# A fused decoder layer: the order of VectorE's, ScalarE's and GpSimd's work from a scheduler with a simulated timeline

## The chip, the cores and the metric

The kernel runs on one core of one Trainium2 chip, as one program. The metric is the device time of that core in microseconds (us); the number for a kernel is the median over several executions. A profile is one further execution taken by the hardware profiler. A core has a matrix engine (TensorE, in the profile PE, its weight loads PEld), VectorE (DVE), ScalarE (ACT), GpSimd (POOL) and a queue that issues DMAs (SP). Each engine works through its own list of instructions in the order in which the program holds them, and the engines meet through semaphores: an instruction waits until the results that it reads are there and the buffers that it writes are free.

## The reference

The program computes one decoder layer in fp32 for `x` of 32 batches x 100 tokens x 256 and a context of 32 x 361 x 256. Cut to what matters:

```python
x = x + self_attention(layernorm(x))        # 16 heads of 16, causal, rotary q and k, @ Wo.T
x = x + cross_attention(layernorm(x), ctx)  # 16 heads of 16, 361 keys, with biases
x = x + soft_moe(layernorm(x))              # below

def soft_moe(x):                            # 8 experts with 128 slots each, hidden size 1024
    xn, sn = rmsnorm(x) * gamma, rmsnorm(slot_embeds) * gamma2
    logits   = einsum('bnd,esd->bnes', xn, sn)
    dispatch = softmax(logits, over tokens n)
    combine  = softmax(logits, over all slots e,s)
    slots = einsum('bnd,bnes->besd', xn, dispatch)
    eo    = gelu(slots @ w1 + b1) @ w2 + b2   # per expert
    return einsum('bmd,bnm->bnd', eo, combine)
```

## The kernel before, in words

The 32 batches are taken in eight groups of four. For each batch there is self-attention, cross-attention and the token normalization; then, for each group, the eight experts run on the four batches' slots together. While the experts of one group run, the attention of the next group's batches is woven in between their matmuls. Only the first group's attention (with the constants) has no experts beside it, and only the last group's experts have no attention beside them. In the profile this gives a start and a preparation of 291 us, six nearly equal periods of 396 us, and an end without attention.

TensorE's order is written out by the kernel itself. Generators (`self_attention`, `cross_inputs`, `cross_softmax`, `prepare`, `route`) yield points in an estimate of TensorE's time, and `between`, called inside `run_expert`, decides which generator may put its next matmuls there. The helpers `matmul` (line 88) and `transpose` (line 92) wrap each TensorE instruction in `tc.keep_in_program_order`, which binds its place. All matmuls therefore appear in the profile under line 88, all transposes under line 92, and are told apart by their tiles.

The instructions of VectorE, ScalarE and GpSimd have no such binding. A scheduler takes the traced program and lays each engine's list out, subject to data and buffers; it also places the semaphore waits.

The steps that the prediction names, by tile and line:

- Start: the context copies `ctxT` (L547) and the slot normalization `sq` (L264, eight squares with a sum each), `n` (L265), `rn` (L267, GpSimd), `se` (L269, eight), `ps_sn` and `snT` (L282). `wTWo` (L202) is a weight turned by TensorE.
- Every layer norm: `bnmv` (L308), then on GpSimd `ve`, `rstd`, `xh` (L310 to L318); TensorE turns it into `ps_xhT`, ScalarE copies that into `xhT` (L330).
- Self-attention: `ps_qk`, then the rotation `ropeu`, `ropet` (L392 to L395, VectorE and GpSimd) and `rotk` (L398, ScalarE); `spad` (L410) holds the values. The scores `sc` are masked into `p` (L430), reduced to `nmax` (L436), shifted on GpSimd (L437), raised by Exp (L441, written `p<-p`), summed (`sums`, L442), inverted (`rinv`, L444) and widened (`wide`, L344). TensorE turns `p` into `ps_pT`, copied to `pT` (L460).
- Cross-attention: `ps_kT` and `kT` (L559), `vpad` (L573), `ps_xq` and `xqT` (L589), scores `xsc`, `xnmax` (L607), Exp `xp` (L611), turned into `ps_xpT` and copied to `xpT` (L627 on ScalarE, L629 on VectorE); `rb` (L354) is the spread inverse of the sums.
- Experts: routing makes `dT` and `cT` (Exp at L824 and L825, `sm` L827, `ri` L829), `disp` (L836) and `slT` (L848); `ph` is the first expert product, Gelu writes `hT` (L873), `pe` is the second product, `eo` (L890) takes it out, `py` combines, and L903 adds it to `x` (called the combine).

PSUM has one tile of four banks for scores, two banks "mm" and two "big", which `ph` and `pe` share with other work; a matmul that needs a bank waits for the copy that empties it.

## Time and profile before

| | |
|---|---|
| median of 3 runs (lowest, highest) | 3293.3 us (3292.8, 3299.66) |
| profiled execution, and its span in the profile | 3290.16 us, 3288.4 us |
| TensorE busy, share of the span | 3080.1 us, 94% |
| ScalarE busy | 1447.5 us, 44% |
| VectorE busy | 1292.9 us, 39% |
| GpSimd busy | 555.5 us, 17% |
| table loads on ScalarE | 272 of 1283 ns |
| mean granted TensorE clock | 0.98 |

How to read it: a busy TensorE does not mean TensorE at its peak, since its matmuls overlap and their ends are modelled. In a line of the profile "out<-in" names the tiles, "x4096" is a count, then come the busy time, the mean of one, and the idle time of that engine just ahead with what ended it. "PE ps_qk L88 <- ACT xhT L330" is TensorE, at the product `ps_qk`, waiting for ScalarE's `xhT`. In a timeline the first number is the start from the span's beginning, the second the duration of the merged pieces, and a bracket holds the idle time before them.

### The profile page before, as it was taken

The page shows a single profiled execution, that of the slowest core. Times are in us where ns is not written, and L with a number is a line of the kernel's source. Part 1 is how long each engine was busy: PE and PEld are TensorE (multiplying, and loading weights), DVE is VectorE, ACT ScalarE, POOL GpSimd, SP SyncE. Part 2 cuts the span into 40 slices and gives each one's busy share as a digit, 9 for nine tenths or more (in the row PEclk, how much of TensorE's full clock was granted, in tenths as well). Part 3 has the DMA queues.
Part 4 walks back from the last instruction along what each step waited for, and adds up shares of the span by engine and source line. Part 5 has one row for each costly group of instructions (what it writes and reads, how often), then busy time and mean ns, then how long its engine had stood idle before and what let it go on. Part 6 is the DMA issues. An engine that isn't in the chain of part 4 may idle for free.

```text
span 3288.4 us, 44719 instructions
## 1 busy us (share of the span) xinstructions
PE 3080.1 (94%) x18481; PEld 2126.4 (65%) x18481; DVE 1292.9 (39%) x2477; ACT 1447.5 (44%) x2824; POOL 555.5 (17%) x816
## 2 busy tenths in 40 slices
PE   5778999999999999999999999999999999999999
PEld 3556666666666666666666666766666666666666
DVE  3554444433443443434443343443443433422211
ACT  2444445344454445444445345444445444534331
POOL 3231211103101121112211011210211102000000
PEclk9788999999999999999999999999999999999999
DMA  3000111111111111112111111112111111111121
GB/s 107 10 10 13 47 49 56 47 51 60 47 45 59 52 45 64 47 43 67 47 45 52 60 45 59 47 45 65 47 45 48 57 48 55 42 63 64 63 64 55
DMA packets 116316, 167.51 MB, mean 51 GB/s; under 512 B 4521, under 2 KB 99729, under 8 KB 116113
## 3 DMA queue, kind: packets, MB, share of 16 engines
q1 hardware_dynamic: 112368, 161.01, 15.1%
q10 hardware_dynamic: 3744, 3.65, 0.4%
q8 instruction: 145, 2.38, 0.3%
q14 instruction: 59, 0.48, 0.0%
HBM read 161.36 MB, written 3.28 MB: 50 GB/s over the span
## 4 chain that ended last, share of the span: by engine, by line
PE 80%; ACT 9%; DVE 5%; POOL 4%; issue 2%; DMA 0%; ACTq 0%; DVEq 0%; POOLq 0%
PE ph L88 24%; PE pe L88 24%; PE sl L88 3%; PE ps_xpT L92 3%; PE xsc L88 3%; PE ps_lt L88 2%; PE ps_xv L88 2%; PE py L88 2%; PE ps_xav L88 2%; PE ps_kT L88 2%; ACT L873 2%; PE ps_o L88 2%; ACT hT L873 2%; POOL p L437 1%; ACT xp L611 1%
## 5 line engine op out<-in xcount | busy, mean ns | idle before, releaser
L88 PE MATMUL pe<-w,hT 128*128 128x256 f32 x4096 | 1048.3, 386 | 1.8 <-ACT hT L873 1.8
L88 PE MATMUL ph<-slT,w 128*128 128x512 f32 x2048 | 994.4, 602 | 25.3 <-ACT hT L873 24.6
L88 PEld LDWEIGHTS pe<-w,hT 128*128 128x128 f32 x4096 | 734.8, 191 | 170.3 <-issue 73.1
L873 ACT ACTIVATE hT<-ph,cols 128x512 f32<-128x512 f32 x512 | 350.3, 687 | 486.7 <-PE ph L88 480.8
L88 PEld LDWEIGHTS ph<-slT,w 128*128 128x128 f32 x2048 | 357.2, 190 | 291.1 <-issue 224.8
L611 ACT ACTIVATE xp<-xsc,xnmax 100x361 f32<-100x361 f32 x512 | 282.9, 558 | 263.6 <-DVE xnmax L607 262.8
L607 DVE TENSOR_REDUCE xnmax<-xsc 100x2 f32<-100x722 f32 x256 | 231.7, 905 | 250.6 <-PE xsc L88 172.8
L92 PEld LDWEIGHTS ps_xpT<-ident,xp 100*128 100x128 f32 (+1 forms) x1536 | 183.7, 157 | 120.9 <-issue 63.3
L629 DVE COPY xpT<-ps_xpT 128x400 f32<-128x400 f32 (+1 forms) x256 | 145.1, 570 | 261.8 <-PE ps_xpT L92 261.2
L830 POOL TENSOR_TENSOR dT<-dT,ri 128x400 f32<-128x400 f32 x64 | 55.3, 864 | 1012.3 <-DVE ri L829 968.5
L92 PE MATMUL ps_xpT<-ident,xp 100*128 100x100 f32 (+1 forms) x1536 | 203.9, 260 | 19.8 <-ACT xp L611 9.6
L873 ACT ACT_TABLE_LOAD x136 | 174.5, 1283 | 83.1 <-PE ph L88 81.3
L890 DVE TENSOR_TENSOR eo<-pe,b 128x512 f32<-128x512 f32 x128 | 88.2, 689 | 279.9 <-PE pe L88 279.3
L823 POOL TENSOR_TENSOR cT<-lt,nmB 128x400 f32<-128x400 f32 x64 | 66.2, 1039 | 679.9 <-ACT nmB L810 354.3
L903 DVE SCALAR_TENSOR_TENSOR x<-py,cinv,x 100x256 f32<-100x256 f32 x256 | 112.1, 479 | 164.5 <-PE py L88 163.6
L88 PEld LDWEIGHTS sl<-disp,xn 100*128 100x128 f32 x1024 | 133.9, 194 | 20.9 <-ACT rb L354 8.0
L88 PE MATMUL sl<-disp,xn 100*128 100x128 f32 x1024 | 137.3, 278 | 9.1 <-ACT rb L354 5.2
L437 POOL TENSOR_TENSOR p<-p,nmax 100x800 f32<-100x800 f32 x64 | 96.1, 1523 | 249.9 <-DVE nmax L436 239.5
L88 PE MATMUL py<-eo,cT 128*100 128x256 f32 x512 | 131.8, 380 | 0.8 <-DVE eo L890 0.8
L88 PE MATMUL xsc<-kT,xqT 32*100 32x361 f32 x1024 | 112.8, 510 | 10.4 <-ACT xp L611 9.5
L848 DVE TENSOR_SCALAR slT<-sl,cols 128x512 f32<-128x512 f32 x128 | 95.5, 746 | 65.0 <-PE sl L88 64.4
L310 POOL TENSOR_SCALAR ve<-bnmv 100x1 f32<-100x1 f32 x96 | 21.4, 223 | 582.7 <-DVE bnmv L308 579.2
(143 smaller groups left out, 3416.6 us busy)
## 6 DMA issues: line engine op xcount, KB each, us to landing
w<-in_L_ffn_w_dram SPq DMA_DIRECT2D x128, 1024.0 KB
ctx<-in_ctx_dram SPq DMA_DIRECT2D x32, 256.0 KB
b<-in_L_ffn_b_dram SPq DMA_DIRECT2D x64, 128.0 KB
ctx<-in_ctx_dram SPq DMA_DIRECT2D x32, 105.0 KB
x<-in_x_dram SPq DMA_DIRECT2D x8, 400.0 KB
out_dram<-x SPq DMA_DIRECT2D x16, 200.0 KB
se<-n_L_ffn_slot_embeds_dram ACTq DMA_DIRECT2D x1, 1024.0 KB
rawWk<-in_L_attn_Wk_dram ACTq DMA_DIRECT2D x1, 256.0 KB
```

The lines of the kernel that those rows point to most:

```text
L88: tc.keep_in_program_order(nc.tensor.matmul(out, lhsT=lhsT, rhs=rhs, **kw))
L92: tc.keep_in_program_order(nc.tensor.transpose(out, in_, identity))
L437: nc.gpsimd.tensor_tensor(p[:, hs, :], p[:, hs, :], nmax[:, hs].unsqueeze(2).to_broadcast([S, HPC, S]), ALU.subtract,)
L607: nc.vector.tensor_reduce(nmax[:, c, q : q + 2, r], sc[:S, q : q + 2, :SK], axis=AX.X, op=ALU.max, negate=True,)
L611: nc.scalar.activation(p[:, q, :], sc[:S, q, :SK], AF.Exp, bias=nmax[:, c, q, r : r + 1], accum_out=sums[:, c, q, r : r + 1],)
L629: nc.vector.tensor_copy(pT[:n], ps[:n, : HG * S])
L823: nc.gpsimd.tensor_tensor(cT, k.lt[e], k.nmB, ALU.add)
L830: nc.gpsimd.tensor_tensor(dT, dT, ri.unsqueeze(2).to_broadcast([P, nb, S]), ALU.mult)
L848: nc.vector.tensor_scalar(slT[:, dc, :], sl[:, : nb * NS], cols[:, NGM + dc : NGM + dc + 1], None, ALU.mult)
L873: nc.scalar.activation(h[:, :n], ph_[:, :n], AF.Gelu, bias=cols[:, e * NHC + hc : e * NHC + hc + 1])
L890: nc.vector.tensor_tensor(eo[:, :m], po[:, :m], b2.unsqueeze(1).to_broadcast([P, m, D]), ALU.add)
L903: nc.vector.scalar_tensor_tensor(xg[g][:, b, :], py[:S, i, :], k.ci[:, b : b + 1], xg[g][:, b, :], ALU.mult, ALU.add,)
```

## The change

One argument at the place where the program is made:

```diff
-    with _tile.TileContext(nc) as tc:
+    with _tile.TileContext(nc, schedule_with_timeline_sim=True) as tc:
         decoder_layer(tc, aps, *outs)
```

With it the scheduler keeps a simulated timeline while it lays the lists out, so that the instruction taken next on an engine follows that timeline's idea of what is ready. The traced program is the same, instruction by instruction. What differs is the order on three engines and, with it, where the semaphore waits stand: TensorE's list is the same; 537 of VectorE's 2445 instructions, 285 of ScalarE's 2017, 425 of GpSimd's 813 and 4 of SP's 280 stand in another place. Four excerpts of ScalarE's list, old and new, with the times that the places had in the profile before:

```
start (20 to 43 us)
  old: ctxT x2, sq x8, xhT, rotk x2, spad, kT x2
  new: ctxT x2, xhT, rotk x2, sq x7, spad, sq, kT x2
preparation (242 to 248 us)
  old: Exp p, Exp p, xhT, xnT, xp, xp
  new: xhT, xnT, xp, xp, Exp p, Exp p
period (345 to 356 us)
  old: hT, xhT, Exp cT, hT, hT, rotk x2, spad
  new: hT, xhT, hT, Exp cT, hT, spad, (hT,) rotk x2
period (517 to 530 us)
  old: hT, xp, xp, ctxT, ctxT, Exp p, xpT, Exp p, kT
  new: hT, ctxT, xp, xp, ctxT, xpT, kT, Exp p, Exp p
```

On VectorE the commonest moves are of neighbours: `xpT` ahead of `nmax` or `sums`, `xqT` or `xnmax` ahead of `wide`, `ri` and `sm` ahead of `slT`, the combine ahead of `nmax`. On GpSimd the short layer norm steps `ve`, `rstd`, `xh` pass the token normalization's chain (L729 to L737), which was interleaved with them.

## The prediction

> **What bounds the kernel now.** I read the busy totals and the chain first, then who TensorE waits for, then the stretches.
>
> ```profile
> PE 3080.1 (94%) x18481; PEld 2126.4 (65%) x18481; DVE 1292.9 (39%) x2477; ACT 1447.5 (44%) x2824; POOL 555.5 (17%) x816
> PE 80%; ACT 9%; DVE 5%; POOL 4%; issue 2%; DMA 0%; ACTq 0%; DVEq 0%; POOLq 0%
> ```
>
> TensorE (PE) is busy 3080.1 of 3288.4 us; 208 us are gaps. Its own work isn't touched, so a gain can only come out of those gaps, and a loss can only be a new gap. The other three engines idle for over half the time: their amount of work doesn't bind, the moment at which each result is ready does. TensorE's waits, longest first (who waits, for whom: us in total, times, longest):
>
> ```profile
> PE ps_qk L88 <- ACT xhT L330: 25.8, 3, 21.8
> PE ph L88 <- ACT hT L873: 24.6, 21, 1.7
> PE ps_l L92 <- ACT ps_l L795: 23.1, 7, 3.6
> PE ps_rb L92 <- DVE wide L344: 13.9, 3, 6.5
> PE ps_xq L88 <- ACT xhT L330: 11.8, 3, 5.3
> ```
>
> Many short waits in many places, and one long one. The stretches (us: TensorE busy, the number of its instructions; then the clock and the DMA columns at the end):
>
> ```profile
> 0.00:57.00 57.00, 22.20 (x153) 17.72 (x153) 19.15 (x41) 12.76 (x35) 17.91 (x31) 0.95 0.48 147
> 57.00:291.00 234.00, 175.38 (x1561) 129.12 (x1554) 135.51 (x267) 102.45 (x288) 71.28 (x103) 0.83 0.03 9
> 687.00:1083.00 396.00, 380.84 (x2307) 262.06 (x2306) 160.65 (x307) 183.29 (x353) 68.61 (x100) 0.99 0.16 52
> 3007.00:3289.00 282.00, 266.65 (x1050) 184.06 (x1050) 51.54 (x97) 83.51 (x106) 13.36 (x14) 1.00 0.19 63
> ```
>
> Gaps: 35 us in the start (7 of them for the first weights' DMAs, 22 at `ps_qk`), 59 us in the first group's preparation, where no expert runs beside it, 15 us in each later period of 396 us, 15 us in the last experts.
>
> [...] on ScalarE `xhT` needed only `ps_xhT`, done at 11.45, and went at 32.89, after eight squares that waited for the DMA of `se`:
>
> ```profile
> 21.86 0.82 ACT L547 COPY ctxT<-ps_cT 128x361 f32<-128x361 f32 x2
> 29.69 0.42 ACT L264 ACTIVATE sq<-se 128x256 f32<-128x256 f32 x1 [7.00 <-DMA se<-n_L_ffn_slot_embeds_dram]
> 32.89 0.30 ACT L330 COPY xhT<-ps_xhT 128x200 f32<-128x200 f32 x1
> ```
>
> [...] the trace has 1283 x272. [...] the trace shows one `wide` copy at 1.13 us against a mean of 0.32, beside GpSimd. A new order can move such clashes; I take zero and keep 0.8 us for each of five to ten either way (4 to 8 us) for the range.
>
> **The change, part by part.** No instruction is added or removed. TensorE's order is the same. Of VectorE's 2445 instructions 537 stand in another place, of ScalarE's 2017 285, of GpSimd's 813 425, most by one to four places; of SP's 280 DMAs 4 (the third ctx load passes x and b, nothing waits there). The 272 table loads stay, with the same number ahead of each line. So cost is only lateness: I keep every TensorE start where the trace has it, lay the other queues out in the new order with each instruction's duration from the trace, starting it when its queue and its inputs are done (handover 0.03 to 0.09 us, as the trace shows), and read how much earlier or later TensorE's operand is than before. The same layout in the old order makes nothing late by over 0.05.
>
> *Start.* `xhT` goes ahead of the squares: 22.7 to 23.0 instead of 33.2, so `ps_qk` and the rotation start 10.3 earlier. The squares now stand behind `rotk` (two, 29.6 to 30.4) and the last one behind `spad`: the chain square, n2, rn (1.67), se (8, 2.19) ends 1.0 later. `ps_sn` follows se directly, its first at 36.4, its last at 39.3 instead of 44.1, so `sc` comes 4.7 earlier. VectorE's `wTWo` (0.68) now stands ahead of `nmax`, hidden again by the earlier `wide`. Kept: 4.4 us.
>
> *Preparation.* The clearest place is 246.6:
>
> ```profile
> 243.97 0.87 ACT L441 ACTIVATE p<-p 100x800 f32<-100x800 f32 x1 [4.37 <-POOL p L437]
> 245.45 0.87 ACT L441 ACTIVATE p<-p 100x800 f32<-100x800 f32 x1 [0.61 <-POOL p L437]
> 246.22 0.31 ACT L330 COPY xhT<-ps_xhT 128x200 f32<-128x200 f32 x1
> ```
>
> `xhT`, ready at 240.2, waited behind two Exps that waited for GpSimd; it now goes first, and the stall of 3.5 us at `ps_qk` goes. At 276.2 `xhT` likewise (2.6, but the second Exp falls behind a `pT` copy and gives 1.7 back: 0.9); at 71.9 the four `xqT` ahead of `sums` and `rinv` (1.5); at 99.5 the cross Exps and their `xnmax` ahead of `pT` and `xqT` (2.7); at 225.2 the same with `rotk` (2.1). Five smaller gains of 0.2 to 0.5: 1.6. Seven losses of 0.1 to 0.8, the largest `ropeu` behind a 0.91 `xnmax` at 221: 2.6. Net 9.7.
>
> *Periods.* The largest gain:
>
> ```profile
> 347.85 1.28 ACT L825 ACT_TABLE_LOAD   x1
> 351.16 0.54 ACT L825 ACTIVATE cT<-cT 128x400 f32<-128x400 f32 x1 [2.02 <-POOL cT L823]
> 351.71 1.28 ACT L873 ACT_TABLE_LOAD   x1
> 353.01 1.26 ACT L873 ACTIVATE hT<-ph,cols 128x512 f32<-128x512 f32 x2
> ```
>
> The first of these two Gelus (its `ph` was done long before) now goes ahead of the Exp that waited for GpSimd, so TensorE's 1.54 stall at 353.7 goes. Beside it:
>
> ```
> place (and each 396 us on)   what passes what                        us, times      sum
> 331  sl                      xnmax ahead of ri                       +0.61 x7      +4.3
> 354  ph                      hT ahead of Exp cT                      +1.53 x6, .94 +10.1
> 434  ps_xpT                  combine x, xpT ahead of nmax, Exp p     +0.92 x6      +5.5
> 521  sc                      two cross Exps sooner                   +0.38 x6      +2.3
> 526  ps_xpT, ps_kT           xpT ahead of nmax and Exp p       +1.7, +0.24 x5      +2.9
> 535  py                      Exp p behind kT, so sums, disp, eo late -1.10 x6      -6.6
> 692  ph                      sm (0.57) ahead of slT                  -0.31 x6      -1.9
> ```
>
> Sum +16.6. The loss at 535: Exp `p` at 526.07 now stands behind `kT`, which waits for `ps_kT` until 528.9, so it and all behind it are 3.3 late; 2.2 of that is covered by slack at `py`:
>
> ```profile
> 526.07 0.87 ACT L441 ACTIVATE p<-p 100x800 f32<-100x800 f32 x1 [4.80 <-POOL p L437]
> 528.89 0.56 ACT L559 ACTIVATE kT<-ps_kT,cols 128x361 f32<-128x361 f32 x1 [0.47 <-PE ps_kT L88]
> ```
>
> *End.* +1.0 at 2854.6 (combine ahead of other work), -0.5 at 2966.3; the last five stalls of 1.67 stay. Net +0.5.
>
> Elsewhere moves cost nothing: `sm`, `ri` ahead of `slT` in about 25 experts lie under 1.2 to 12 us between the second `slT` and its `ph`. The DMAs follow TensorE's progress and are no later relative to it; no TensorE wait after 8.3 us is for a DMA.
>
> Sum: 4.4 + 9.7 + 16.6 + 0.5 = 31.2. Against the profiled execution's 3290.2: 3259. The median of the runs is 3.1 higher: 3262. A gain at one place survives to the next unless a chain begun before it ends within its slack; laying the gains out as earlier TensorE starts, only the losses named came up.
>
> **Rivals.** (a) The gaps come back: TensorE reaches the next operand earlier and waits for it, as in the preparation, where it waits for VectorE, ScalarE and GpSimd in turn. For: its gaps there are a quarter of the time. Against: most chains start at TensorE and move with it. Half kept: 3293 - 16 = 3277. (b) Nothing measurable: the engines are 39% and 44% busy, so order is of no account. Against: the `xhT` line, 22 us at one place in an idle queue. About 3292. (c) Slower: `rotk` (L398) now stands behind `spad` and `hT`, which wait for TensorE, in 19 of 32 batches; it ends up to 2.5 later. For: `sc` waits for it, and all of self-attention behind that. Against: `sc` starts 3.3 to 12.3 after `rotk` ends. Without that cover 19 x 2.5 = 47 against 31: 3293 + 16 = 3309. It decides above (31.2 + 6.6)/19 = 2.0 uncovered each.
>
> **How the numbers follow.** No change is within 0.2% (6.6 us). Forecast 3254 to 3269: 0.72; (a) 3270 to 3282: 0.16; (b) 0.06; (c) 0.06. Forecast and (a) are both faster: 0.88. Range 3250 [...] to 3278 (most of (a)).
>
> **What would show it.** `xhT` at about 23 and `ps_qk` just behind; no stall at 246 or 354; a new one of about 1 us at `py` near 535; TensorE's gaps about 177 instead of 208, its busy time as before. It is wrong if a new wait of `sc` for `rotk` appears, if a period isn't shorter by about 2.3 us, or if gaps in the preparation stay at 59.

## The result, and the profile after

The changed kernel takes 3254.0 us in the median of four runs (3250.9 to 3259.1), the kernel before 3295.6 in the runs beside them: a ratio of 0.9878, with a 95% interval of 0.9861 to 0.9895. The forecast was 3262, the range 3250 to 3278. The profiled execution took 3259.1 us (span 3257.4), and the forecast for it was 3259.

So the profiled execution became 31.0 us shorter and the median 41.6. The kernel before's profiled execution (3290.2) lies 5.5 below its median and the changed one's 5.1 above its own: 31.0 + 5.5 + 5.1 = 41.6. Why one execution stands off its median by that much is taken up under "The start, and the clock".

Busy totals and the shares of the chain that ended last, of the changed kernel:

```profile
PE 3078.0 (94%) x18481; PEld 2119.3 (65%) x18481; DVE 1284.2 (39%) x2477; ACT 1448.9 (44%) x2824; POOL 553.2 (17%) x816
PE 84%; ACT 8%; DVE 5%; issue 2%; POOL 1%; DMA 1%; ACTq 0%; DVEq 0%; POOLq 0%; SPq 0%
```

TensorE's busy time is 2.1 us less than before, its gaps (the time in which it is idle) are 179.4 us (3257.4 - 3078.0) instead of 208.3. GpSimd has gone from 4% of the chain to 1%. TensorE's waits (who, for whom: us in total, times, longest):

```profile
PE ps_l L92 <- ACT ps_l L795: 22.8, 7, 3.6
PE ps_kT L88 <- ACT kT L559: 15.2, 7, 2.5
PE ph L88 <- ACT hT L873: 15.0, 13, 1.7
PE ps_qk L88 <- ACT xhT L330: 14.8, 2, 14.4
PE ps_xq L88 <- ACT xhT L330: 6.0, 3, 5.2
...
PE ps_sn L92 <- DVE se L269: 4.3, 1, 4.3
...
PE ps_xpT L92 <- DVE xqT L589: 2.8, 6, 0.5
```

`ps_qk` has given 11.0 us, `ph` 9.6 (eight waits fewer), `ps_xq` 5.8. New are `ps_sn` for `se` and `ps_xpT` for `xqT`. The two longest rows that come back in every period, `ps_l` (23.1 before) and `ps_kT` (15.2 before), are nearly as they were. At the places at 246, 348 to 353 and 526 to 529 us that the prediction shows of before, ScalarE's timeline now reads (the second Exp of the pair at 246 is merged with the first, at 234.95):

```profile
230.67 0.33 ACT L330 COPY xhT<-ps_xhT 128x200 f32<-128x200 f32 x1 [0.55 <-PE ps_xhT L92]
...
234.95 1.88 ACT L441 ACTIVATE p<-p 100x800 f32<-100x800 f32 x2
...
333.91 0.69 ACT L873 ACTIVATE hT<-ph,cols 128x512 f32<-128x512 f32 x1 [0.56 <-PE ph L88]
334.62 1.28 ACT L825 ACT_TABLE_LOAD   x1
335.91 0.54 ACT L825 ACTIVATE cT<-cT 128x400 f32<-128x400 f32 x1
...
512.45 0.56 ACT L559 ACTIVATE kT<-ps_kT,cols 128x361 f32<-128x361 f32 x1 [3.91 <-PE ps_kT L88]
512.91 1.62 ACT L441 ACTIVATE p<-p 100x800 f32<-100x800 f32 x2
```

`xhT` goes ahead of the Exps. One Gelu passes the Exp of `cT`, and that Exp doesn't wait for GpSimd any more. `p` stands behind `kT` and is late, as forecast. (Below, "the place at 354" means the instructions that stood there in the profile before, and the same ones each 396 us on.) The same stretches as before (us, TensorE busy and number of instructions, then the other engines, the granted clock, DMA):

```profile
0.00:57.00 57.00, 25.58 (x153) 19.71 (x153) 18.65 (x42) 12.15 (x35) 17.88 (x31) 0.89 0.51 147
57.00:291.00 234.00, 184.86 (x1605) 134.07 (x1606) 139.85 (x276) 109.23 (x297) 75.16 (x107) 0.84 0.03 9
687.00:1083.00 396.00, 382.92 (x2315) 262.19 (x2314) 159.49 (x307) 184.50 (x355) 68.41 (x100) 0.99 0.16 52
```

The start has 3.4 us more TensorE busy time, but at a clock of 0.89 instead of 0.95; the preparation has 49 us of gaps instead of 59.

TensorE's list is the same in both kernels, so its idle time can be compared instruction by instruction. In gaps alone (idle time just ahead of each instruction, changed kernel minus kernel before):

```
stretch                         forecast    measured
start (0 to 57)                   -4.4        -3.9   (-7.4 at ps_qk, +4.3 at ps_sn)
preparation (57 to 291)           -9.7        -9.3
six periods                      -15.1       -14.3   (-3.8 in the first, -2.1 in each later one)
the rest                          -2.0        -1.3
sum                              -31.2       -28.8
```

(The forecast's 331 and 354 count a seventh time in the rest: 0.61 + 0.94 of its 16.6, and 0.5 for the end.) Busy time gives the other 2.1.

### The profile page after: what moved, and what is told of

The parts are those of the page before. It is cut to its first block, busy times and chain, and to the rows that moved or that the text cites. A ratio compares the mean times of both kernels' runs of the same rounds, so it can differ in the third digit from the quotient of the medians.

```text
span 3257.4 us, 44717 instructions
## 1 busy us (share of the span) xinstructions
PE 3078.0 (94%) x18481; PEld 2119.3 (65%) x18481; DVE 1284.2 (39%) x2477; ACT 1448.9 (44%) x2824; POOL 553.2 (17%) x816
## 3 DMA queue, kind: packets, MB, share of 16 engines
q1 hardware_dynamic: 112368, 161.01, 15.4%
## 4 chain that ended last, share of the span: by engine, by line
PE 84%; ACT 8%; DVE 5%; issue 2%; POOL 1%; DMA 1%; ACTq 0%; DVEq 0%; POOLq 0%; SPq 0%
PE ph L88 26%; PE pe L88 25%; PE ps_xpT L92 4%; PE sl L88 3%; PE py L88 3%; PE xsc L88 3%; PE ps_lt L88 3%; PE ps_xv L88 2%; PE ps_xav L88 2%; PE ps_kT L88 2%; PE ps_o L88 2%; PE ps_qk L88 2%; ACT L873 1%; ACT hT L873 1%; PE ps_pT L92 1%
## 5 line engine op out<-in xcount | busy, mean ns | idle before, releaser
L823 POOL TENSOR_TENSOR cT<-lt,nmB 128x400 f32<-128x400 f32 x64 | 66.3, 1042 | 661.1 <-ACT nmB L810 345.4
L627 ACT COPY xpT<-ps_xpT 128x400 f32<-128x400 f32 x128 | 62.7, 490 | 176.9 <-PE ps_xpT L92 176.6
L88 PEld LDWEIGHTS py<-eo,cT 128*100 128x100 f32 x512 | 84.9, 167 | 55.6 <-issue 31.6
```

Of the source, the lines that this page charges most:

```text
L88: tc.keep_in_program_order(nc.tensor.matmul(out, lhsT=lhsT, rhs=rhs, **kw))
L627: nc.scalar.copy(pT[:n], ps[:n, : HG * S])
L823: nc.gpsimd.tensor_tensor(cT, k.lt[e], k.nmB, ALU.add)
```

## The experiments

TensorE's list stays the same in all kernels but one, which adds transposes. To set another engine's order, each of the kernels e1 to e11 writes it out and binds every instruction behind the one before it (shortened):

```diff
     with _tile.TileContext(nc) as tc:
         decoder_layer(tc, aps, *outs)
+        for engine, order in ORDERS.items():          # positions in the traced program
+            mine = [i for i in nc.cur_bb.bb.instructions if i.engine == engine]
+            for a, b in zip(order, order[1:]):
+                tc.add_manual_dep(mine[b], mine[a].name, NO_SYNC, reason="pin")
```

The scheduler's timeline is off in them, but for e9 and e12. "Old" and "new" below are the lists of the kernel before and of the changed one. All results together, with two columns that the first experiments called for: TensorE's busy time and gaps in the profiled execution, and the number of steps at half clock in it ("half steps"), counted from 20 us on. Each ratio is against runs of the kernel before that stand beside the kernel's own. (A step is 3.413 us: so long are the shortest whole stretches at 0.5 in the profiles of before and changed, and in the records of the granted clock of every one of these profiles, all stretches at 0.5 from 100 us on begin at whole multiples of 3.413 us from each other, to 0.01 of a step.)

```
kernel                              median    ratio (95%)             span     busy     gaps   half steps
before                              3295.6    1                       3288.4   3080.1   208.3    39
changed                             3254.0    0.9878 (0.9861-0.9895)  3257.4   3078.0   179.4    36
e1  ScalarE new, periods            3300.3    1.0009 (1.0000-1.0018)  3297.0   3091.7   205.3    46
e2  VectorE new, periods            3323.0    1.0073 (1.0047-1.0100)  3312.3   3089.2   223.1    43
e3  GpSimd new, periods             3298.5    1.0002 (0.9992-1.0011)  3297.4   3094.5   202.9    48
e4  all new, preparation            3280.3    0.9945 (0.9925-0.9965)  3278.9   3076.5   202.4    36
e5  ScalarE+VectorE new, periods    3287.1    0.9966 (0.9953-0.9978)  3281.9   3082.9   199.0    43
e6  changed, three places mended    3251.4    0.9863 (0.9846-0.9879)  3247.3   3075.5   171.8    38
e7  changed, two ScalarE moves      3221.0    0.9767 (0.9753-0.9782)  3218.5   3070.9   147.7    31
e8  changed, ps_sn wait filled      3265.3    one run                 3263.4   3086.9   176.4    40
e9  changed, 66 moves               3200.3    0.9714 (0.9700-0.9729)  3197.8   3063.8   134.0    30
e10 before, two ScalarE moves       3258.2    0.9889 (0.9874-0.9903)  3257.7   3077.6   180.1    40
e11 new order, buffers by old rule  3263.1    0.9899 (0.9881-0.9918)  3261.8   3082.5   179.3    41
e12 changed, once more              3258.9    one run                 3257.2   3079.7   177.5    35
```

### One engine at a time, in the periods

e1, ScalarE's list, in each period (all but the place at 434, whose new order needs VectorE's):

```diff
-hT, Exp cT, hT           | rotk x2, spad, hT | xp, xp, ctxT | Exp p, xpT, Exp p, kT
+hT, hT, Exp cT           | spad, hT, rotk x2 | ctxT, xp, xp | xpT, kT, Exp p, Exp p
```

> ScalarE alone in the new order, from 291 us to the end of the periods (2700), all its moved places but the one at 434 (xpT ahead of two Exp p, which VectorE's old order doesn't allow). VectorE, GpSimd and all other stretches in the old order. Theory (ScalarE's order carries the places 354, 521, 526 and the loss at 535): 354 -10.1, 521 -2.3, 526 about -1.5, 535 +6.6, so about 7 us less than the kernel before; TensorE's wait of ph for hT at 354 is gone and py at 535 waits about 1 us. Rival (GpSimd's order does it, below): only the loss at 535 shows, 3 to 7 us more than before. Rival (clock): the number of stretches at half clock changes and the total moves by up to 8 us beyond these, either way.

e2, VectorE's list (excerpts):

```diff
-nmax, nmax, xpT          | xqT x4, xrinv, xpT, wide | slT, sm, slT, ri
+xpT, nmax, nmax          | xrinv, wide, xqT x4, xpT | sm, slT, ri, slT
```

> VectorE alone in the new order, from 291 to 2700; ScalarE and GpSimd in the old one. Theory (VectorE carries 331, 434, 692 and the loss at 573 seen in the changed kernel): 331 -4.3, 434 -5.5 if xpT isn't held by ScalarE's old place for its own xpT behind the Exps, 692 +1.9, 573 +3.8: about 4 us less than before. Rival (434 needs both engines, so that part is missing): 1 to 5 us more than before.

e3, GpSimd's list: the steps of `cT` (L823) and of the layer norm pass the token normalization's.

> GpSimd alone in the new order, from 291 to 2700; ScalarE and VectorE in the old one. Theory (my sum names no place where GpSimd's order matters): no change, within 4 us of before, and the wait of ph for hT at 354 still 1.5 us. Rival (the Exp of cT at 354 is late only because GpSimd has its cT behind other steps, so GpSimd's order alone removes the wait): that wait is gone and the time is 10 to 16 us less than before.

A whole list new over all stretches, beside old ones, wasn't tried: the lists then wait for each other in a ring, as at 434. In the gaps of the six periods: ScalarE alone -2.6 us, VectorE alone +13.8, GpSimd alone -5.0. Their sum is +6.2, while all three together in the changed kernel give -14.3.

At 354, ScalarE's order alone takes the whole 1.54 away in all six periods, as I had it. So does GpSimd's alone, as the rival had it. Timeline of GpSimd at that place in the kernel before, then in e3 (start, duration):

```profile
346.26 1.24 POOL L737 TENSOR_SCALAR xn<-x,bnmv,r 100x256 f32<-100x256 f32 x1
...
350.10 1.03 POOL L823 TENSOR_TENSOR cT<-lt,nmB 128x400 f32<-128x400 f32 x1
```

```profile
351.19 1.25 POOL L318 TENSOR_SCALAR xh<-x,bnmv,rstd 100x256 f32<-100x256 f32 x1
352.55 1.05 POOL L823 TENSOR_TENSOR cT<-lt,nmB 128x400 f32<-128x400 f32 x1
...
357.07 1.25 POOL L737 TENSOR_SCALAR xn<-x,bnmv,r 100x256 f32<-100x256 f32 x1
```

In the old order `xn` (1.24) and its chain stood ahead of `cT`. Now they follow, `cT` is ready when ScalarE reaches the Exp, and the Gelu behind it comes in time in its old place. One wait had two sufficient cures. Of the 9.2 us gained there in six periods, 1.2 come back at the `ps_xpT` behind it, and 2.9 at 526 in two periods. The time of e3 stays the same: its profile has 5.4 us of gaps less and 14.4 us of busy time more, with nine more half steps than in the profile of before.

With VectorE's order alone the place at 434 gives its 0.89, as forecast. But where VectorE puts `xpT` ahead of `nmax`, ScalarE still has its own `xpT` behind an Exp `p` that waits for `nmax` by way of GpSimd. Timeline of e2, ScalarE and then TensorE, at this place in the third period (near 535 in the first; in brackets the idle time and what ended it):

```profile
1331.39 0.87 ACT L441 ACTIVATE p<-p 100x800 f32<-100x800 f32 x1 [5.28 <-POOL p L437]
1332.17 0.47 ACT L627 COPY xpT<-ps_xpT 128x400 f32<-128x400 f32 x1
...
1332.69 1.48 PE L88 MATMUL ps_kT<-ctxT,xwWk 128*128 128x361 f32 x4 [2.39 <-ACT xpT L627]
```

`ps_kT` waits for that copy to empty its bank. In the kernel before the same wait is 0.24; here it is 0.8 to 2.4 in the later periods (0.73 instead of 0.90 in the first), 7.4 us more in all. 354 gets 0.81 worse in each period, the context transposes near 438 lose 0.5. Neither theory had that: mine said -4 us, the rival +1 to +5; measured are +14.7 in gaps and +0.73% in time.

ScalarE alone keeps the gain at 354 but pays 3.7 at a `ps_kT` and 4.4 at `py` (expected 6.6 there), so 3.0 of the 7 us come in gaps, and with seven more half steps the time rises by 0.09%.

### ScalarE and VectorE together

> ScalarE and VectorE in the new order from 291 to 2700, GpSimd and all other stretches in the old one. In gaps of TensorE (its idle time, clock left aside) the changed kernel saves 14.4 us in these six periods. Theory (the places of the periods need ScalarE's and VectorE's order together, and GpSimd's order adds nothing to them): gaps of the periods 12 to 15 us less than before, 331, 354, 434 all gone. Rival (GpSimd's order is needed as well): at most half of it, 0 to 7 us less. The total moves by that plus 1.2 to 1.7 us for each stretch at half clock more or less.

-11.3 us in the gaps of the periods, -9.3 in all, and 0.9966 in time: the theory, just under its lower end. (The 1.2 to 1.7 us for a stretch at half clock was my estimate; the profiles of e1 and e3 have 11.6 and 14.4 us more busy time than that of before, with seven and nine more half steps, and all fourteen give 1.46 each, below.) The loss of e2 turns into a gain once ScalarE's `xpT` passes Exp `p` too. What is missing against -14.3 is one place, `sl` at 331: -0.19 a period here, -0.70 in the changed kernel.

### The order alone

> All three engines in exactly the changed kernel's order, but with the scheduler's timeline off, so that the buffers (which of the four PSUM banks and SBUF slots a tile gets) are laid out by the old rule. Theory (the order gives the gain, the banks only the 0.5 us at sl in each period, where sl doesn't stand in the bank of ps_rb): gaps 25 to 26 us less than the kernel before, 3 to 4 less gain than the changed kernel, sl waiting for rb 0.5 us in seven places. Rival (the buffers carry a large part of the gain): 10 us or more of it missing. Rival (no part): the same as the changed kernel within 1 us of gaps.

The rest at `sl` isn't the order. With the changed kernel's lists on the three engines, every instruction in its place, `sl` waits for `rb` (waits of the kernel before, then of e11 and, in the same way, of e6, e7 and e8; the changed kernel has no such row):

```profile
PE sl L88 <- ACT rb L354: 5.2, 7, 0.7
```

```profile
PE sl L88 <- ACT rb L354: 3.8, 7, 0.5
```

`rb` is no operand of `sl`. It is the copy that empties the bank of `ps_rb`, which `sl` is to write. In the programs as built, 1246 of 5749 tiles lie in another slot in the changed kernel than in the kernel before, 814 of them in PSUM, 78 tiles named `sl` among them: the scheduler gives a tile its slot while it lays the lists out. So the change has a third part beside order and waits. In gaps it is worth what the theory said, 0.5 in each of seven places; the other places of the periods are equal. (In sum the gaps are 179.3 against 179.4, since the start of this execution is some 3 us better: `xhT` went at 22.95 us instead of 25.93.) e11 isn't a kernel with the slots of the kernel before: its slots are laid out by the old rule for the new lists. e11 has five more steps at half clock, and its time (0.9899) can't be told apart from the changed kernel's (0.9878).

### The preparation

```diff
 ScalarE, 242 to 248 us of the kernel before, as one excerpt of three lists
-Exp p, Exp p, xhT, xnT, xp, xp
+xhT, xnT, xp, xp, Exp p, Exp p
```

> All three engines in the new order from 57 to 291 us alone (the preparation), the old one elsewhere. Theory: the gaps of the preparation shrink from 59 us to about 46 and the total by 10 (my sum) to 13 (the shift seen in the changed kernel), and the rest keeps its time. Rival (the gain of one stretch is given back later): the preparation is shorter but the total is the same as before.

Gaps of the preparation -8.8 us, of everything else +2.6 (0.8 in the start, 1.5 in one period); the profiled execution 9.6 us shorter and the median 15.4. So most of the gain stays.

### The start, and the clock

In the changed kernel TensorE idles for 4.3 us ahead of `ps_sn`, and then is slow:

```profile
26.33 2.03 PE L88 MATMUL ps_qk<-xhT,wTWq 128*128 128x100 f32 x8 [14.39 <-ACT xhT L330]
...
39.63 4.02 PE L92 MATMUL ps_sn<-ident,se 128*128 128x128 f32 x16 [4.28 <-DVE se L269]
43.58 1.56 PE L88 MATMUL sc<-rotk,ropet 32*100 32x200 f32 x16
```

The same two steps in the kernel before:

```profile
42.18 1.91 PE L92 MATMUL ps_sn<-ident,se 128*128 128x128 f32 x16
44.02 0.94 PE L88 MATMUL sc<-rotk,ropet 32*100 32x200 f32 x16
```

e8 fills the wait:

```diff
         ps = bank("ps_sn")
+        for j in range(34 if dc == 0 and e0 == 0 else 0):
+            tc.keep_in_program_order(nc.tensor.transpose(ps[:, :NS], ident, ident))
```

> The changed kernel with 34 more transposes of the identity into the ps_sn bank, ahead of the sixteen real ones, where TensorE idles 4.3 us for se (a unit of work that isn't in the reference; the real ones write over it). Theory (the idle 4.3 us lets the clock fall to half just as ps_sn starts, so what the start gained is lost there): with the wait filled, the clock stays at 1.0 from 35 to 45 us, the sixteen transposes take 1.9 us instead of 4.0 and sc starts 2 to 4 us sooner than in the changed kernel. Rival (the clock falls for another reason): they still take 4 us, and sc is no sooner or up to 4 us later.

Timeline of TensorE in e8:

```profile
34.30 3.87 PE L277 MATMUL ps_sn<-ident 128*128 128x128 f32 x34
38.01 1.91 PE L92 MATMUL ps_sn<-ident,se 128*128 128x128 f32 x16
39.85 0.94 PE L88 MATMUL sc<-rotk,ropet 32*100 32x200 f32 x16
```

The clock is 1.00 from 34.3 to 44.8 us (in the changed kernel it is 0.50 from 38.1 to 44.9), the transposes take 1.91, and `sc` starts 3.7 us sooner than in the changed kernel. Of these 3.7 us, 2.8 are another thing: `xhT` went at 23.1 instead of 25.9, behind ScalarE's 17 DMA issues, which were done sooner in this execution. Counted from `xhT`, `sc` comes 0.9 sooner and the next `ps_qk` 1.6. That it is the fill which keeps the clock up, and not the earlier `xhT`, the six profiles with the new order in the start and no fill show (the changed kernel, e6, e7, e9, e11, e12): there the transposes take 3.77 to 4.02 us, with `xhT` at 22.7 to 25.9. The total of this run is no shorter: 40 steps at half clock, 36 in the changed kernel's profile.

I laid every 3.413 us step from 305 us on, in all fourteen profiles, over TensorE's idle time. After a step at full clock with over 2.01 us idle the next one was at half clock in 113 of 113 cases, with 1.36 to 2.01 in 24 of 243, with less in none of 11591 (in the profiles of before and changed alone: 19 of 19, 2 of 42, none of 1653). After a step that was itself at half clock, the next one was at half clock too in 15 of 15 cases with 0.74 us or more idle, in 1 of 138 with less. These are counts of these profiles; what lowers the clock they don't show. Behind a wait of 2.45 us the clock differed with how the wait lay on the steps. At `ps_kT` in the changed kernel 2.11 us of it lay in the step from 447.69 us, 0.35 in the next one, and that one was at half clock (two stretches in a row; behind the busy times stands the clock, 0.98 and then 0.51):

```profile
447.80:451.20 3.40, 1.19 (x7) 0.68 (x4) 0.00 (x0) 3.37 (x7) 0.00 (x0) 0.98 0.69 276
451.20:454.60 3.40, 3.15 (x6) 1.84 (x6) 0.00 (x0) 0.67 (x3) 0.00 (x0) 0.51 0.00 0
```

In the kernel before, the same wait of 2.45 lay in two steps with 1.66 and 0.80 us, and the step behind each was at full clock:

```profile
464.50:467.90 3.40, 1.73 (x9) 1.06 (x7) 0.00 (x0) 3.36 (x6) 0.00 (x0) 1.00 0.94 292
467.90:471.30 3.40, 2.61 (x14) 1.32 (x14) 0.00 (x0) 1.43 (x5) 0.00 (x0) 1.00 0.04 17
```

Over the fourteen profiles, busy time goes with the number of half steps: about 3024 us + 1.46 each, all within 5.1 us (correlation 0.94, e8's 3.9 us of extra work taken off). The 30 to 48 half steps are 44 to 70 us in all. That is the second part of every time here, beside the gaps. It accounts for what e3's shorter gaps didn't bring: over its twelve runs the mean granted clock is 0.9757, over the 23 runs of the kernel before beside them 0.9778. That is about four half steps, 6 us at 1.46 each (an estimate), against 5.4 us of gaps.

> The changed kernel once more, to see how far one profile stands for the kernel. Theory (what varies from run to run are ScalarE's DMA issues in the start and where the waits fall against the steps of the clock): TensorE's gaps from 57 us on the same within 1 us, the start's gaps up to 4 us less with xhT at 22 to 23 us, and its busy time off by up to 10 us with the number of stretches at half clock. Rival (the gaps themselves vary): gaps after 57 us off by 3 us or more.

e12 is the changed kernel, run again. The gaps from 57 us on are the same to 0.1 us; the start has 1.8 less, most of it at `ps_sn` (`xhT` was again late, at 25.6), and busy time is 1.7 more. In this one repeat, then, the gaps behind the start are a property of the kernel. The half steps came out nearly alike (35 and 36).

The spread of a kernel's time goes with the clock too. The record has the mean granted clock of every run. In the 39 runs of the kernel before that stand beside e1 to e12, it lies between 0.974 and 0.980: at 0.974 and 0.975 the time is 3302.2 us on average (8 runs), at 0.980 3292.0 (8 runs). The profiled execution of before, at 0.980, is one of the quickest of its kernel, and the changed kernel's is the slowest of its four (0.982, the others 0.982 and 0.983). From 0.978, the median of the 39, to the changed kernel's 0.9825 is eight or nine half steps, 12 to 13 us at 1.46 each (an estimate); with 28.9 us of gaps that is about the 41.6 us between the medians. The start adds to the spread: its gaps in the changed kernel's lists differ by up to some 3 us from one execution to another. All this is a correlation; no experiment sets the clock alone over a whole kernel.

### Places mended

```diff
 in each period, from the changed kernel's lists
-ScalarE  xpT, kT, Exp p, Exp p                 VectorE  xrinv, wide, xqT x4, xpT | sm, slT, ri, slT
+ScalarE  xpT, Exp p, Exp p, kT                 VectorE  xqT x4, xrinv, xpT, wide | slT, sm, slT, ri
```

> The changed kernel with three losing places mended in each of the six periods: kT behind the two Exp p again at 535 (xpT stays ahead of them), the four xqT ahead of xrinv and wide at 573, slT ahead of sm and ri at 692. Theory (each loss is what its place shows in the trace): TensorE's waits at py, ps_xpT and ph shrink by 0.63, 0.47 and 0.32 a period, 8 us in all, and 3246 us. Rival (the new order as a whole needs these places, so that other waits take over): gaps unchanged, time within 3 us of the changed kernel's 3254.

The three waits shrink by 3.4, 2.8 and 1.9 us, 8.1 us in all, as expected, with 0.8 more at two `ps_kT`; the buffers' 0.5 at `sl` comes on top seven times, since the scheduler's timeline is off here too. The time (0.9863) can't be told from the changed kernel's: 3 of the expected 8 us, 38 half steps instead of 36.

### The two longest waits

```diff
 ScalarE, seven places of the first and six of the second, from the changed kernel's list
-Exp ps_l, Gelu hT, Exp ps_l                   hT, Exp xp, Exp xp, kT
+Exp ps_l, Exp ps_l, Gelu hT                   hT, kT, Exp xp, Exp xp
```

> The changed kernel with two moves on ScalarE, at the two longest waits that both kernels share: the second Exp of ps_l directly behind the first, where a Gelu with two table loads stood between them (seven places), and kT ahead of the two Exp xp (seven places). Theory (these waits, 22.8 and 15.2 us in the changed kernel, are only a matter of ScalarE's order, and they are also what puts TensorE to half clock in the periods): the two waits go, gaps 30 to 38 us less, stretches at half clock after 291 us from 11 to 4 or fewer, TensorE's busy time 8 to 12 us less, in all 3254 - 44 = 3210 us, between 3204 and 3222. Rival (half clock has other causes): gaps shrink but the number of stretches and the busy time stay, 3218 to 3226. Rival (the delayed Gelu or Exp now stops TensorE): 3240 or more.

Timeline of ScalarE and then TensorE in e7, at the first `ps_l` of the periods:

```profile
648.30 1.09 ACT L795 ACTIVATE ps_l<-ps_l,cnm 100x1024 f32<-100x1024 f32 x1
...
649.53 1.09 ACT L795 ACTIVATE ps_l<-ps_l,cnm 100x1024 f32<-100x1024 f32 x1
...
650.79 1.41 PE L92 MATMUL ps_l<-ident,lt 128*100 128x128 f32 x11 [0.29 <-ACT ps_l L795]
```

The wait of 3.57 is 0.29; that of `ps_kT` is gone at the six places, with 0.59 more at the `xsc` behind each. Gaps are 31.7 us less than the changed kernel's, 27.3 of them behind the start, a little under the 30 to 38 expected; the rest is in the start, where nothing was moved (earlier DMA issues). After 291 us there are five half steps instead of eleven, and busy time is 7.1 less: 3221.0, in the forecast's range though 11 over its centre. The rival that half clock has other causes falls.

The same two moves in the old order:

> The kernel before, in its old order, with only the two moves on ScalarE (second Exp of ps_l behind the first, seven places; kT ahead of two Exp xp, six places). Theory (they are independent of the scheduler's change): the same 31 us of gaps less as in the changed kernel, and 33 in all with the fewer stretches at half clock: 3297 - 33 = 3264, between 3256 and 3270. Rival (in the old order other waits stand right behind these): under 20 us, 3277 or more.

-28.2 us of gaps (31 expected) and 0.9889 in time. Two kinds of move at thirteen places, read off the waits, are worth as much as the whole change (0.9878), and the two gains together give e7 (0.9889 x 0.9878 = 0.9768, measured 0.9767). What is moved is another thing than what the scheduler moved: these two waits are in both kernels.

### A version that beats both

> The changed kernel with 66 single instructions moved ahead by one to eight places, on ScalarE and VectorE nearly all: the two moves of the longest waits, and Gelu or Exp p ahead of work that isn't due, xqT and slT ahead of sums that nothing waits for yet. Worked out from the durations of the changed kernel's trace as in the prediction: 55 us less in gaps than the changed kernel, 16 more than the two moves alone. Theory (gaps are a matter of order, and fewer of them leave fewer stretches at half clock): 3254 - 55 - 5 to 10 = 3192, between 3185 and 3205. Rival (what is moved ahead makes other work late that the durations don't show): 3215 to 3225, no better than the two moves alone.

An excerpt of the moves in the last experts, where ScalarE went back and forth between its tables (1.28 us a load, as at 334.62 above):

```diff
-Gelu hT, Exp cT, Gelu hT, Gelu hT
+Gelu hT, Gelu hT, Exp cT, Gelu hT
```

3200.3 us, 0.9714 of the kernel before and 1.7% under the changed kernel. Gaps are 45.4 us less than the changed kernel's (expected 55), half steps 30. What came short is mostly in the last experts: the wait of 1.67 at `ph` went five times, and came back as 1.25 one product later. That is the rival, at one place of many.

## Why the prediction was right or wrong

*What bounds.* Right for the profiled execution: the gain came out of TensorE's gaps (208.3 - 179.4 = 28.9 of 31.0 us), and its busy time changed by 2.1. That this execution was met to 0.1 us (3259 and 3259.1) is luck: the gaps gave 2.3 less than forecast, and busy time, which was to stay, made up for it. Of the 41.6 us between the medians some 13 are more than these gaps; they go with the granted clock, of which the forecast said nothing.

*Start.* The gain in gaps was near (-3.9 for -4.4), though `xhT` went 3 us later than forecast in this one execution (22.7 to 23.1 in e6, e7 and e8). "`ps_sn` follows se directly, its first at 36.4, its last at 39.3" was right in its first time (36.37 in e6) and wrong in what follows: behind the new wait of 4.28 us ahead of `ps_sn` the clock was 0.50, which the prediction left out. The sixteen took 4.02 us instead of 1.91. At 57 us TensorE stood 0.5 us ahead of the kernel before in the profile of the changed kernel, 1.0 in e12, 3.6 to 3.8 in e6, e7 and e11.

*Preparation.* Right: 9.3 for 9.7, 8.8 when done alone, and most of it stays.

*Periods.* The sum was right (16.0 for 16.6, the last 331 and 354 with it). By place: 354 -1.54 (-1.53), 434 -0.89 (-0.92), 521 -0.23 (-0.38), 535 +0.63 (+1.10), 692 +0.32 (+0.31); 573, which I had let go as covered, +0.47. Two reasons in the table were wrong or half right. At 331 "xnmax ahead of ri" gives 0.19 of the 0.70; the other 0.51 is a PSUM bank, and I hadn't looked whether buffers move. That the table's 0.61 came near was luck. At 354 "hT ahead of Exp cT" is enough alone, but so is GpSimd's order, of which I said nothing. Nor did the table say that its places hold only together; VectorE's alone cost 13.8.

*"If a period isn't shorter by about 2.3 us."* In gaps it is 2.1; in time the later periods lost 3.5, the rest being fewer half steps (one a period instead of two).

*From the profile to the median.* "The median of the runs is 3.1 higher" was the step that failed in size: it took the offset of one kernel's single profile for a constant. The median lies 5.5 above the profiled execution for the kernel before, with four runs, and 5.1 below it for the changed one. The forecast of 3262 took +3.1 where -5.1 was measured; these 8.2 us are the whole of its miss.

*Rivals.* (a) the gaps come back: no, e4 and the table of gaps; (b) no difference: no; (c) `rotk` late: no wait of `sc` for `rotk` appears, so the cover of 3.3 us and more held. The slow `wide` copies beside GpSimd, for whose moves the prediction took zero and kept 4 to 8 us either way, came out as a small gain. In the kernel before, eight of the 96 `wide` copies are slower than the rest (0.45 to 1.13 us, the others at most 0.30), 2.4 us in all, and each began while a GpSimd operation ran and ended 0.08 to 0.15 us behind it. In the changed kernel none is; in e2 and e5, with VectorE's new order in the periods, two are left. The one that the prediction mentions held TensorE up. `wide` with GpSimd's `ropet` and TensorE's `ps_rb`, before and then changed:

```profile
53.86 1.03 POOL L395 TENSOR_TENSOR ropet<-ropet,ropeu 128x400 f32<-128x400 f32 x1 [1.56 <-DVE ropet L393]
53.91 1.13 DVE L344 COPY wide<-rinv 100x256 f32<-100x256 f32 x1
55.09 0.59 PE L92 MATMUL ps_rb<-ident,wide 100*128 100x100 f32 x2 [1.15 <-DVE wide L344]
```

```profile
52.75 1.03 POOL L395 TENSOR_TENSOR ropet<-ropet,ropeu 128x400 f32<-128x400 f32 x1
53.92 0.29 DVE L344 COPY wide<-rinv 100x256 f32<-100x256 f32 x1
54.37 0.57 PE L92 MATMUL ps_rb<-ident,wide 100*128 100x100 f32 x2 [0.16 <-DVE wide L344]
```

That is 1.0 us of the start's 3.9. No experiment moves this copy alone.

## What to carry to other kernels

Where one engine binds and its list is fixed, compare its idle time instruction by instruction: that is what an order is worth. Behind the start it repeated to 0.1 us in the one repeat made here, while the total of one execution lay up to 5.5 us off its median. Orders of several engines are one thing: VectorE's new list beside the others' old ones made gaps 14.7 us longer, though it was worth having beside ScalarE's new one. Before changing a scheduler, read the few longest waits that repeat and ask what stands ahead of the releaser: thirteen moves gave as much as a scheduler's 1250.

## What was not expected of the hardware

In these profiles a 3.413 us step at full clock with over 2.01 us of TensorE idle time was followed by one at half clock in 113 of 113 cases, with 1.36 to 2.01 us in 24 of 243; a half step went with about 1.46 us more busy time. The wait of 2.45 us at `ps_kT` was followed by one in the changed kernel (2.11 us of it in one step), and by none in the kernel before (1.66 and 0.80). Behind a step at half clock with 0.74 us or more idle the next was at half clock too, in 15 of 15 cases. A VectorE copy `wide`, 0.29 us in the changed kernel at 53.92, took 1.13 in the kernel before while a GpSimd operation ran. ScalarE's last DMA issue of the start ended at 20.5 to 23.9 us from one execution to another, and in the five profiles of the new order in which its end was read (the changed kernel, e6, e7, e8, e12) `xhT` began 2.0 us after it.
